# A graph network's two layers on one core: TensorE's steps ordered behind the counting, and the opening loads reordered

## The chip, the cores and the metric

The kernel runs on one core of a Trainium2 chip. The metric is the device time of one execution in microseconds (us). Before the change three executions took 1819.74, 1822.57 and 1822.67 us; the median is 1822.57. The engines are named as in the profile: PE (TensorE, matrix products), DVE (VectorE), ACT (ScalarE), POOL (GpSimd, which issues the indirect loads) and SP (which issues most other transfers).

## The reference

The input is a graph of 2500 nodes with 1024 features each, and 80,000 edges sorted by destination. Two layers follow each other, each with a residual:

```
h   = relu(layernorm(x))
x   = x + segment_sum((h @ W0)[src] * edge_weight[:, None], dst)
h   = relu(layernorm(x))
deg = 1 + number of edges of each dst;   n = deg ** -0.5
x   = x + segment_sum over the edges and self loops of n[dst] * n[src] * (h @ W1.T + b)[src]
```

The first layer needs a gather of rows by `src`, a weight per edge, and a sum by `dst`. The second needs only how often each pair (dst, src) occurs, since its weight is a product of a factor per row and a factor per column.

## The kernel before

**Tiles and blocks.** Nodes are cut into 20 tiles of 128 rows. Edges of a destination tile are cut into blocks of 128: TILE_BLOCKS gives 146 for tile 0, 62, 48, 41 for tiles 1 to 3, down to 10 for tile 19, 675 in all.

**Opening (L149 to L351).** w0 is loaded by eight 512 KB transfers from ACT's queue (L170). Rows of x and columns of its transpose xT come from SP (L145, L154). For each node tile `transposed_rows` takes mean and variance (L126, L128), subtracts the mean from xT through a small product (L160 to L163) and applies ReLU (L164). Beside it a chain of small steps on DVE, PE and POOL finds where each tile's edges start (`heads` L179, L203, L209, L220), gathers the edges by block (`got` L245), transposes them (L263), finds each block's first row (L288, L289) and makes `low` and `key`, the two numbers of an edge from which it is counted.

**Support (L450 to L469).** For each of the 20 node tiles, 16 products with w0 (L453), a scaling by ACT (`row`, L467) and a store to `support` in DRAM (L468).

**Counting (`count_group`, L361 to L402).** For each block DVE makes two one-hot matrices (`oh_low` L380, `oh_key` L382) and PE multiplies them (L384): the counts of source rows against a short window of destination rows, of WINDOWS columns for each source tile. Two to four blocks make a group, and DVE adds the group's result into the tile of counts (L391) at a position read from memory. For the four tiles with most edges (DENSE = 4) ACT also makes three weighted one-hots per block (`wl`, L388), PE multiplies those (L395), and DVE adds them into a dense matrix of edge weights (L398). When a tile is complete it is added to `total` (L401) and stored to DRAM (`cnat`, L402). A new tile of counts is zeroed by ACT (L366; dense L370); there are three buffers of counts, four of each one-hot (pool `ohs`, L115), and two PSUM tiles `cb` for the groups.

**First layer's sums (L501 to L530).** Destination tiles are taken in the order ORDER = 3, 4, 5, 6, 2, 7, 8, 9, 1, ... The four dense ones multiply their dense matrix with rows of `support` read by SP (`multiplied`, L526, L528). The others (`gathered`) take, block by block, 128 rows gathered by POOL (L506), a one-hot (L510), the weighted rows split into two parts (`hi` on ACT L512, `lo` on DVE L514), and four products (L518). Each tile is finished while the next one runs (`finish`, L484 to L499): residual, norm, transposition (L478), 16 products with w1 (L453 again), bias and store.

**Second layer (L580 to L617).** All rows are split into `hi` and `lo`, and each tile's counts, read back transposed (L593), are multiplied with them: 1600 products (L613).

**What sets the order.** The program is written in one order, and a scheduler places the instructions on each engine by data dependences, buffers and its own costs; each engine then runs its list in that order. Where counting is put among the other work is decided in the source by a small model: `clock` holds a time for PE, DVE and ACT, `takes` adds the cost of a step, and `count` (L434), called after each step, adds groups until DVE or ACT would be later than PE. Two lists wait for it: groups of the dense tiles and groups of the others. `least` sets how many blocks of the second may still be open.

Of the kernel before, what the change touches and what calls it, by code (L numbers as in the profile page):

```python
# [9 lines left out]
F32 = mybir.dt.float32  # L10
# [24 lines left out]
LEAD = 4.0  # L35

# [4 lines left out]
def direct(  # L41
# [73 lines left out]
    ohs = first.enter_context(tc.tile_pool(name="ohs", bufs=4))  # L115
    cpool = first.enter_context(tc.tile_pool(name="cpool", bufs=3))
    wpool = first.enter_context(tc.tile_pool(name="wpool", bufs=1, reuse_waits="tile"))
    sup_ctx = tc.tile_pool(name="sup", bufs=3, side="right")
# [30 lines left out]
    def transposed_rows(t):  # L149
        xt = load_rows(t, sup)  # L150
        hT = sup.tile([P, KC, P], F32, name="hT")
        if rows(t) < P:
            nc.gpsimd.memset(hT, 0.0)
        nc.sync.dma_start(hT[:, :, :rows(t)], xT[:, t * P:t * P + rows(t)].rearrange("(k p) n -> p k n", p=P))  # L154
        mv = moments(xt, sup)
# [11 lines left out]
    def load_w(w, engine):  # L167
        ws = [wpool.tile([P, D], F32, name=f"w{k}") for k in range(KC)]
        for k in range(KC):
            engine.dma_start(ws[k], w[k * P:(k + 1) * P, :])  # L170
            yield ws

    for w0_sb in load_w(w0, nc.scalar):
        pass
    ready = {t: transposed_rows(t) for t in range(2)}


    heads = prep.tile([BP, BC, 1], I32, name="heads")
    nc.sync.dma_start(heads, dst.rearrange("(p c e) -> p c e", p=BP, e=P)[:, :, 0:1])  # L179
# [63 lines left out]
    for c in range(QC):  # L243
        n = min(P, NBP - c * P)
        nc.gpsimd.indirect_dma_start(  # L245
            out=got[:n, c].rearrange("p e q -> p (e q)"), out_offset=None, in_=table,
            in_offset=bass.IndirectOffsetOnAxis(ap=edge_i[:n, c:c + 1], axis=1))
    got_f = prep.tile([P, 2, QC, P], F32, name="got_f")
# [30 lines left out]
    for t in range(2, NT):  # L279
        n = TILE_BLOCKS[t] // 2  # L280
        v = second[:, K0[t] - K0[2]:K0[t] - K0[2] + 2 * n].rearrange("p (n g) -> p n g", g=2)
        nc.gpsimd.memset(v[:, :, 1], 1.0)
    first_row = prep.tile([P, NBP], F32, name="first_row")
    for a in range(0, NBP, 4 * P):
# [4 lines left out]
        nc.vector.tensor_scalar(first_row[:, a:a + n], ps[:, :n], 0.0, float(P - 1), op0=ALU.max, op1=ALU.min)  # L289
# [65 lines left out]

    bases = {}
    dense = {}
    counts = {}
    AW = P + 28

    def count_group(t, g, a, b):  # L361

        w = WINDOWS[t][1]
        if t not in counts:
            counts[t] = cpool.tile([P, NT, AW], F16, name="counts")
            nc.scalar.copy(counts[t].rearrange("p t w -> p (t w)"), zero.to_broadcast([P, NT * AW]))  # L366
            nc.vector.tensor_copy(counts[t][:, t, :rows(t)], ident[:, :rows(t)])
            if t < DENSE:
                dense[t] = dpool.tile([P, NT, P + 12], F32, name="dense")
                nc.scalar.copy(dense[t].rearrange("p t w -> p (t w)"), zero.to_broadcast([P, NT * (P + 12)]))  # L370
# [588 lines left out]
```

## Time and profile before

| what | us |
|---|---|
| median of three executions | 1822.57 |
| profiled execution, its own time | 1826.62 |
| its span, first to last instruction | 1824.6 |
| first product L453 / first counting product L384 | 23.5 / 77.3 |
| last weighted one-hot L388 (ACT) | 411 |
| first dense product L528 / first gathered product L518 | 465.6 / 545.3 |
| last product with w1, about | 1437 |
| busy: PE, DVE, ACT, POOL | 1692.6, 1214.6, 911.3, 500.2 |

The table is read as a row of stages: opening, support with counting, first layer's sums, second layer. The span and the events are of the profiled execution, whose time is 4 us above the median. A busy share over the whole span mixes stages with different limits, and the busy time of PE contains records of products that stand in its pipeline and wait.

### The profile page before, as it was taken

How to read it: one execution, taken by the hardware profiler on the slowest of the kernel's cores; microseconds unless marked ns; L12 is line 12 of the kernel's file. 1: busy time of each engine (PE TensorE's matmuls, PEld its weight loads, DVE VectorE, ACT ScalarE, POOL GpSimd, SP SyncE). 2: the span in 40 equal slices, each digit the busy share in tenths (PEclk: the TensorE clock that was granted, in tenths of full speed). 3: DMA queues.
4: the chain of work that ended last, by engine and by line, in shares of the span. 5: the costliest groups of instructions: out<-in, count | busy, mean ns of one | idle time of the engine just before them, and what ended most of it. 6: DMA issues, size and time to landing. Idle time of an engine off the chain costs nothing. (4 is left out here: it accounts for less than half of the span.)

```text
span 1824.6 us, 21434 instructions
## 1 busy us (share of the span) xinstructions
PE 1692.6 (93%) x6506; PEld 1047.4 (57%) x6506; DVE 1214.6 (67%) x3031; ACT 911.3 (50%) x1475; POOL 500.2 (27%) x437
## 2 busy tenths in 40 slices
PE   3899999999869999899999999998999899999998
PEld 1455555554326555466545555455655468888886
DVE  4777766679879998899979999588886330000000
ACT  2499888893117774276625665156654431111110
POOL 2000000000027771277515674166662000000000
PEclk9999999999878999999999999999999999999999
DMA  9123311114759999789978999889885784242420
GB/s 316 52 73 93 108 56 59 47 31 138 264 150 321 377 351 331 216 308 325 345 243 280 325 322 325 261 297 314 307 294 180 210 210 107 81 109 79 113 61 32
DMA packets 216179, 369.97 MB, mean 203 GB/s; under 512 B 115534, under 2 KB 135000, under 8 KB 216054
## 3 DMA queue, kind: packets, MB, share of 16 engines
q0 software_dynamic: 54832, 199.25, 31.5%
q1 hardware_dynamic: 160070, 165.06, 29.0%
q10 hardware_dynamic: 1152, 4.19, 0.7%
q8 instruction: 54, 0.88, 0.2%
q14 instruction: 71, 0.58, 0.1%
HBM read 300.79 MB, written 54.56 MB: 195 GB/s over the span
## 5 line engine op out<-in xcount | busy, mean ns | idle before, releaser
L506 POOL DMA_INDIRECT msg<-support,src_p x378 | 486.1, 1286 | 505.5 <-PE mm L528 126.7
L512 ACT ACTIVATE hi<-msg,wgt_p 128x1024 fp32r<-128x1024 f32 x378 | 423.4, 1146 | 276.3 <-PE mm L518 191.0
L514 DVE SCALAR_TENSOR_TENSOR lo<-msg,wgt_p,hi 128x1024 fp32r<-128x1024 f32 x378 | 476.6, 1280 | 49.6 <-ACT hi L512 47.5
L453 PE MATMUL mm<-w,hT 128*128 128x512 f32 x640 | 321.7, 612 | 1.1 <-ACT hT L164 1.1
L518 PE MATMUL mm<-lo,oh_r 128*128 128x512 f32 x756 | 282.5, 456 | 33.4 <-DVE lo L514 33.3
L518 PE MATMUL mm<-hi,oh_r 128*128 128x512 f32 x756 | 298.1, 477 | 15.9 <-DVE oh_r L510 8.3
L453 PE MATMUL mm<-w,vT 128*128 128x512 f32 x640 | 307.4, 596 | 0.0
L388 ACT ACTIVATE wl<-oh_low,wpart 128x128 bf16<-128x128 bf16 x891 | 267.2, 388 | 21.2 <-PE cb L395 16.1
L613 PE MATMUL mm<-lo,bT 128*128 128x512 f32 (+1 forms) x800 | 248.4, 393 | 3.5 <-DVE lo L587 3.1
L613 PE MATMUL mm<-hi,bT 128*128 128x512 f32 (+1 forms) x800 | 247.7, 392 | 4.1 <-ACT bT L595 2.0
L601 DVE SCALAR_TENSOR_TENSOR rows<-mm,dis,rows 128x1024 f32<-128x1024 f32 x20 | 25.6, 1283 | 308.0 <-PE mm L613 308.0
L518 PEld LDWEIGHTS mm<-lo,oh_r 128*128 128x128 f32 x756 | 141.3, 199 | 117.2 <-DVE lo L514 75.0
L518 PEld LDWEIGHTS mm<-hi,oh_r 128*128 128x128 f32 x756 | 148.7, 202 | 103.4 <-issue 40.3
L382 DVE TENSOR_SCALAR oh_key<-iota,key 128x200 bf16<-128x200 f16 (+13 forms) x675 | 189.7, 292 | 22.5 <-PE cb L395 22.1
L380 DVE TENSOR_SCALAR oh_low<-iota,low 128x128 bf16<-128x128 f16 x675 | 162.8, 251 | 34.4 <-PE cb L384 19.1
L595 ACT CAST bT<-cT 128x2560 fp32r<-128x2560 f16 x20 | 46.6, 2335 | 261.5 <-PE mm L613 257.7
L453 PEld LDWEIGHTS mm<-w,vT 128*128 128x128 f32 x640 | 121.2, 190 | 89.7 <-issue 75.5
L613 PEld LDWEIGHTS mm<-lo,bT 128*128 128x128 f32 (+1 forms) x800 | 149.6, 188 | 40.3 <-DVE lo L587 9.4
L613 PEld LDWEIGHTS mm<-hi,bT 128*128 128x128 f32 (+1 forms) x800 | 150.3, 189 | 37.8 <-ACT hi L585 2.5
L391 DVE TENSOR_TENSOR counts<-cb,counts 128x220 f32 (+13 forms) x296 | 138.7, 468 | 45.2 <-PE cb L384 38.2
L528 PE MATMUL mm<-msg,dense 128*128 128x512 f32 (+1 forms) x320 | 158.8, 610 | 7.6 <-DMA msg<-support 7.6
L384 PE MATMUL cb<-oh_key,oh_low 128*128 128x200 bf16 (+13 forms) x675 | 148.4, 294 | 18.6 <-DVE oh_key L382 16.3
(139 smaller groups left out, 1079.5 us busy)
## 6 DMA issues: line engine op xcount, KB each, us to landing
msg<-support SPq DMA_DIRECT2D x76, 512.0 KB, 6.0
xt<-in_x SPq DMA_DIRECT2D x38, 512.0 KB, 4.0
cnat<-counts SPq DMA_DIRECT2D x20, 640.0 KB, 4.7
x_d<-xt SPq DMA_DIRECT2D x20, 512.0 KB, 5.4
hid_d<-hn SPq DMA_DIRECT2D x20, 512.0 KB, 5.4
rows<-hid_d SPq DMA_DIRECT2D x20, 512.0 KB, 4.7
rows<-x_d SPq DMA_DIRECT2D x20, 512.0 KB, 4.5
hT<-in_xT SPq DMA_DIRECT2D x19, 512.0 KB, 3.8
```

Of the source, the lines that this page charges most:

```text
L380: nc.vector.tensor_scalar(oh_low, iota16[:, :P], low[:, k:k + 1], None, op0=ALU.is_equal)
L382: nc.vector.tensor_scalar(oh_key[:, :NT * w], iota16[:, :NT * w], key[:, k:k + 1], None, op0=ALU.is_equal)
L384: nc.tensor.matmul(cb[:, :NT * w], oh_low, oh_key[:, :NT * w], start=(k == a), stop=(k == b - 1))
L388: nc.scalar.activation(wl[:, i, :], oh_low, AF.Copy, scale=wpart[:, i, k:k + 1])
L391: nc.vector.tensor_tensor(to, cb[:, :NT * w].rearrange("p (t w) -> p t w", w=w), to, op=ALU.add)
L453: nc.tensor.matmul(mm[:, h, :], vT[:, k, :], ws[k][:, h * H:(h + 1) * H], start=(k == 0), stop=(k == KC - 1))
L506: nc.gpsimd.indirect_dma_start(out=msg, out_offset=None, in_=support, in_offset=bass.IndirectOffsetOnAxis(ap=src_p[:, k:k + 1], axis=0))
L512: nc.scalar.activation(hi, msg, AF.Copy, scale=wgt_p[:, k:k + 1])
L514: nc.vector.scalar_tensor_tensor(lo, msg, wgt_p[:, k:k + 1], hi.bitcast(F32), op0=ALU.mult, op1=ALU.subtract)
L518: nc.tensor.matmul(sums[:, h, :], oh, v[:, h * H:(h + 1) * H], start=(j == 0 and v is hi), stop=(j == n - 1 and v is lo))
L528: nc.tensor.matmul(sums[:, h, :], dense[t][:rows(k), k, :P], msg[:rows(k), h * H:(h + 1) * H], start=(k == 0), stop=(k == NT - 1))
L613: nc.tensor.matmul(mm[:, h, :], bT[:rows(k), k, :], v[:rows(k), h * H:(h + 1) * H], start=(k == ORDER[0] and v is his[k]), stop=(k == ORDE ...
```

## The change

- **Opening loads.** w0 no longer comes from ACT's queue. SP loads `heads` first, then x and xT of tile 0, the first column halves of the eight w0 tiles, x and xT of tile 1, the second halves, and x and xT of tiles 2 and 3. Loads are issued four tiles ahead (`load_tile`), with five buffers for xT and four for x. The program's order has the products of tiles 0 and 1 ahead of the edge transposes.
- **Windows.** A block's first row is held at 128 minus the window's width (`roof`), so that counts need 128 columns where they had 156, and the dense matrices 128 where they had 140. `oh_key` shrinks to 460 columns.
- **Buffers.** The one-hot pool has 8 buffers instead of 4.
- **Order.** `fences` keeps, for each call of `count`, the last counting product so far; `on_pe` orders each later step's product behind the one of five calls ago. The edge is for the scheduler alone; no semaphore comes of it. In `gathered` and `multiplied` the first product of a step carries it.
- **How much is counted when.** Costs in `count_next` and the choice between the two lists change, and counting starts after tile 4 instead of tile 2. In the built order of PE, 66 products L453 stand ahead of the first count (34 before), 500 of the 675 counts ahead of the first dense product (399 before), and 547 ahead of the first gathered one (500 before). The last weighted count stands behind 230 products (282 before).
- **Stores.** A tile of counts is stored six calls of `count` after it is complete, ordered behind the last step's product.

The diff, cut to its core:

```diff
+BEHIND = 5
-    ohs = first.enter_context(tc.tile_pool(name="ohs", bufs=4))
+    ohs = first.enter_context(tc.tile_pool(name="ohs", bufs=8))
-    sup_ctx = tc.tile_pool(name="sup", bufs=3, side="right")
+    sup_ctx = tc.tile_pool(name="sup", bufs=4, side="right")
...
-    for w0_sb in load_w(w0, nc.scalar):
-        pass
-    ready = {t: transposed_rows(t) for t in range(2)}
+    AHEAD = 4
     heads = prep.tile([BP, BC, 1], I32, name="heads")
     nc.sync.dma_start(heads, dst.rearrange("(p c e) -> p c e", p=BP, e=P)[:, :, 0:1])
+    w0_sb = [wpool.tile([P, D], F32, name=f"w{k}") for k in range(KC)]
+    loaded = {}
+    for t in range(AHEAD):
+        loaded[t] = load_tile(t)
+        for k in range(KC) if t < 2 else ():
+            nc.sync.dma_start(w0_sb[k][:, t * H:(t + 1) * H], w0[k * P:(k + 1) * P, t * H:(t + 1) * H])
+    ready = {t: transposed_rows(*loaded.pop(t)) for t in range(2)}
...
+    for t in range(2, AHEAD):
+        ready[t] = transposed_rows(*loaded.pop(t))
+    last_pe = None
+    last_count = None
+    fences = []
+
+    def on_pe(i):
+        nonlocal last_pe
+        last_pe = i
+        if len(fences) >= BEHIND and fences[-BEHIND] is not None:
+            order_behind(i, fences[-BEHIND])
+        return i
+
+    def order_behind(i, other):
+        tc.add_manual_dep(i.ins, other.ins.name,
+                          mybir.DependencyInfo(mybir.DependencyClass.NoSync, mybir.DependencyReason.SCHED_ONLY),
+                          reason="order of the steps")
...
+    for t in range(2):
+        for _ in products(t):
+            pass
...
-        nc.vector.tensor_scalar(first_row[:, a:a + n], ps[:, :n], 0.0, float(P - 1), op0=ALU.max, op1=ALU.min)
+        nc.vector.scalar_tensor_tensor(first_row[:, a:a + n], ps[:, :n], 0.0, roof[:, a:a + n],
+                                       op0=ALU.max, op1=ALU.min)
...
-    AW = P + 28
-            counts[t] = cpool.tile([P, NT, AW], F16, name="counts")
+            counts[t] = cpool.tile([P, NT, P], F16, name="counts")
-                dense[t] = dpool.tile([P, NT, P + 12], F32, name="dense")
+                dense[t] = dpool.tile([P, NT, P], F32, name="dense")
...
-            nc.sync.dma_start(cnat[:, t].rearrange("k p d -> p k d"), counts[t][:, :, :P])
+            to_store.append([6, t])
...
-            takes(0.5 * n, (one + 0.25) * n + 2 * add, 0.92 * n)
+            takes(0.5 * n, 1.2 * (one * n + 2 * add), 0.92 * n)
-            takes((0.05 + 0.0005 * wide) * n, (one * n + add) * 1.3)
+            takes((0.05 + 0.0005 * wide) * n, 1.2 * (one * n + add))
...
+    def store_counts(late=True):
+        for entry in to_store:
+            entry[0] -= 1
+        while to_store and (to_store[0][0] <= 0 or not late):
+            t = to_store.pop(0)[1]
+            i = nc.sync.dma_start(cnat[:, t].rearrange("k p d -> p k d"), counts[t])
+            if late:
+                order_behind(i, last_pe)
+
     def count(pe=0.0, v=0.0, s=0.0, least=None):
+        fences.append(last_count)
         takes(pe, v, s)
+        store_counts()
...
-            dense_first = to_count[0] and (not to_count[1] or clock[S] <= clock[V] + LEAD / 2)
+            dense_first = to_count[0] and (not to_count[1] or clock[S] <= clock[V])
...
-        for _ in product(hT, w0_sb, mm):
-            (count if t >= 2 else takes)(1.75)
+        for _ in products(t):
+            (count if t >= 4 else takes)(1.75)
```

## The prediction

> **What bounds the kernel now.** I read the slices of the page first, because no single share describes a kernel with stages.
>
> ```profile
> PE   3899999999869999899999999998999899999998
> DVE  4777766679879998899979999588886330000000
> ACT  2499888893117774276625665156654431111110
> PEclk9999999999878999999999999999999999999999
> ```
>
> PE is nearly always "busy", which says little: records of a waiting matmul count too. What changes is who else is full. ACT is full in slices 3 to 9 (of 45.6 us), DVE from 10 to 15, and both dip in 11 and 12, where the granted clock falls to 0.7. The last eight slices are the final products L613, which the change leaves alone.
>
> Next I cut the span at events of the timeline: first counting matmul (77.3 us), last weighted one-hot `wl` (411), first dense product L528 (465.6), first gathered product L518 (545.3).
>
> ```profile
> core 0: us, PE busy (x) PEld busy (x) DVE busy (x) ACT busy (x) POOL busy (x), PEclk, DMA share, GB/s
> 0.00:77.30 77.30, 44.24 (x104) 19.93 (x105) 48.42 (x223) 21.33 (x22) 13.14 (x58) 0.93 0.64 218
> 77.30:411.00 333.70, 331.23 (x1726) 191.07 (x1725) 232.94 (x925) 308.54 (x934) 0.95 (x1) 1.00 0.21 64
> 411.00:465.60 54.60, 47.01 (x168) 19.46 (x166) 53.13 (x223) 14.21 (x11) 0.00 (x0) 0.94 0.52 158
> 465.60:545.30 79.70, 63.39 (x181) 24.09 (x181) 65.77 (x255) 13.46 (x6) 8.94 (x8) 0.80 0.63 208
> 526.80:545.30 18.50, 10.21 (x24) 2.51 (x24) 16.70 (x61) 2.79 (x1) 0.00 (x0) 0.50 0.27 64
> 545.30:704.00 158.70, 148.70 (x516) 93.13 (x515) 156.89 (x253) 116.46 (x109) 112.96 (x91) 0.95 0.94 345
> 965.00:1136.00 171.00, 159.19 (x543) 99.59 (x541) 159.04 (x267) 109.11 (x105) 112.65 (x82) 0.95 0.90 316
> ```
>
> The reader is to see four limits in turn: PE half empty in the opening; PE and ACT both full while tiles 0 to 3 are counted with weights; DVE full while the rest is counted (53.1 of 54.6 us); DVE, with the DMA at 0.94, in the gathered tiles. In 526.8 to 545.3, PE has nothing but 24 counting records: 26 counts stand in its order ahead of the first gathered product and come at DVE's pace.
>
> Last, the groups of the stretch 77.3 to 411, ACT and then DVE (busy, mean ns | idle before, ended by):
>
> ```profile
> L388 ACT ACTIVATE wl<-oh_low,wpart 128x128 bf16<-128x128 bf16 x886 | 265.7, 388 | 21.2 <-PE cb L395 16.1 <-DVE oh_low L380 3.7 <-PE cb L384 0.8
> L467 ACT ACTIVATE row<-mm,rstd 128x1024 f32<-128x1024 f32 x14 | 15.4, 1100 | 2.2 <-PE mm L453 2.2
> L164 ACT ACTIVATE hT<-hT 128x1024 f32<-128x1024 f32 x14 | 14.6, 1046 | 1.7 <-DVE hT L163 1.6
> ...
> L382 DVE TENSOR_SCALAR oh_key<-iota,key 128x200 bf16<-128x200 f16 (+2 forms) x312 | 76.4, 269 | 22.5 <-PE cb L395 22.1
> L398 DVE TENSOR_TENSOR dense<-cb,dense 128x200 f32 (+1 forms) x102 | 38.0, 372 | 33.7 <-PE cb L395 33.3
> ```
>
> ACT and DVE stand idle for PE's `cb L395`: products of the support stand ahead of the counts in PE's order, and only four one-hot buffers cover the delay.
>
> **The change, part by part.** The built programs of both kernels give the order of instructions on each engine; I count in it and take durations from the profile. A product L453 is two records, 0.86 us (the chain shows four records in 1.72 us).
>
> *Opening.* w0 goes from ACT's queue (eight issues from 0.7 to 16.8 us) to SP's, in sixteen halves of 256 KB, behind `heads`, x and xT of the tile that needs them. SP issues at about 0.42 us each (the xT issue at 1.2 us), so x, xT and eight halves are out by 6 us; at the 350 GB/s of the windows from 5 to 25 us, the 3 MB take 9 us. ACT first runs a table load more (1.3 us, as the one at 17.2), three zeroings (2.3 each), a root and the first ReLU: first product at about 12 us against 23.5. [...] The row has ten 512 KB loads in flight together at a DMA share of 1.0; I go by the row. The edge chain (`heads` to the six `got` gathers) also moves: its matmul L203, at 23.4 us, now stands behind five products and runs at about 16. But its transposes stand behind 32 products, 12 + 32 x 0.86 = 39.5 us (43.6 before), and the first-row product behind 37, about 47 (55.8). Keys and first one-hots follow after 18.6 us as before (55.8 to 74.4): about 66. First `wl` at 67 instead of 75.9. Before the first count PE has done 66 products instead of 34: 27 us of PE work moved into its empty opening.
> First-row reads the `roof` tile as well (two instructions of 0.5 us) and POOL writes it with 20 memsets (`wide`: 20 in some 2 us, idle POOL): under 1 us, and nothing if POOL stays ahead of the gathers.
>
> *Counting with weights.* ACT now does 891 `wl` (267 us), 11 tiles instead of 14 (2.43 each by rows L467, L164, L157: 26.7), four count zeroings at 2.79 x 2560/3120 = 2.29 and three dense at 2.3 (16): 310 us. With 8 buffers the 16.1 us of waiting for PE should go; the other 9 stay; overlap of successive records takes some 6 off (the groups' busy and idle sum to 341 in a stretch of 334). 313 us: last `wl` at 380 instead of 411. Bounds: 298 (start to start, `wl` at 0.291) and 335 (as now). PE needs 164 products (141), 891 x 0.088 and 375 counts (36): 256 us, so ACT is the limit; DVE goes from 233 to some 265 us (68 further counts at 0.6, three tiles' norms less) and loses idle time.
>
> *The rest up to the gathers.* After the last `wl`, 90 products (77 us) and 113 counts (at 0.13: 15) remain: 92, at 96% 95 us; DVE's 113 x 0.61 = 69 lie beside it (0.61: some 90 counts in 54.6 us). Then the 12 us from the last product to the first dense one, which store and load of `support` take now too (453.8 to 465.6): 12 counts fill it. Then 40 dense products and 47 counts, 34.3 + 6.5 = 41, say 43, instead of 79.7: 54 of its 101 counts stand earlier, and the tail of 26 is gone. First gathered product: 380 + 95 + 12 + 43 = 530 instead of 545.3: 15 us won. With the ends: 365 + 92 + 10 + 41 = 508 and 402 + 100 + 12 + 50 = 564.
> The clock is weighed here. [...] the row has it (0.50 in the tail, 0.80 around it). [...] by the row those gathered products wait for DVE's `lo` anyway (156.9 of 158.7 us), so I credit none.
>
> *Gathered tiles.* Counts left after the first gather: 128 instead of 175. The first two gathered stretches and the dense ones between keep theirs within five. The third (965 to 1136) loses 23, 15 us of DVE; DMA at 0.90 allows about 11 of it, I take 8. The last dense stretch loses 17, 2 us of PE; the other dense ones 1. Sum 11; bounds 0 and 18.
>
> *At nothing:* narrower tiles beyond the zeroings (other strides, same elements); the order fence, which puts no wait into the program; w1's loads, as now. **Late stores:** a store moves by six steps behind its sum, on SP; behind it stand msg loads, x1 and hid stores. It frees one of three count buffers, for which ACT's zeroing waits (118.5 us now, mostly with an idle ACT); two zeroings stand among `hi` after the first and second dense tile, but twelve `hi` stand before the first, more than the store's 4.7 us. If that cover fails, some 5 us each.
>
> **Sum.** 15 + 11 = 26 us off the profiled execution (span 1824.6, 1826.6 with what lies around it): span 1798.6, run 1800.6. The median shown lies 4.0 us lower, so 1796.6: 1797.
>
> **Rivals.**
> *ACT gapless and a full PE:* gather at 508, 18 us from the gathered tiles: 55 off, 1768. For it, 95 us of DVE's idle time in that stretch end with PE; against it, ACT never held more than 48.7 us in 50.
> *Only the opening is won* ([...] or `wl` waits as now): last `wl` at 395 to 402, nothing at the first gather, 11 later: 1812; with a gathered stretch held by the DMA, no change at all.
> *Slower:* PE's order lets steps run only five ahead of the counts, and from tile 8 on each support tile carries some 95 weighted one-hots instead of 55. Where one comes late, the product behind it stands too, then `row`, then ACT, which stands behind `row` itself. Place: 67 to 380. Price: each percent of ACT's share is 3.5 us. At 313 + 26 = 339 us the gain is gone: a share of 310 / 339 = 0.91, where the sum above takes 0.99 and the six ACT groups of the stretch now make 315.5 of 333.7, 0.95. At 0.85: 365 us, 1849. For it: DVE's share rises from 0.70 to 0.85, with two PSUM tiles for the counts; against: ACT and PE together reach 0.92 and 0.99 now.
>
> **How the numbers follow.** The sum 0.50, its own range 1783 to 1810; gapless 0.18; opening only 0.17, a third of it within 0.2%; slower 0.15. 0.2% is 3.6 us, about what a measurement of this kernel tells from no change. Faster 0.50 + 0.18 + 0.11 = 0.79, same 0.06, slower 0.15. Eight in ten: from 1767 (about the gapless case's centre) to 1826, which leaves out part of the slower case.
>
> **What would show it.** First product by 13 us, first `wl` near 67, last near 380, first gathered product near 530, no run of counts alone ahead of it, DVE's waits for `cb` well under 95 us, 11 us less between first gather and last product, final products as before (about 386 us). It is wrong if `wl` ends after 400, if ACT's zeroing stands long in front of `hi`, or if the gathered tiles, whose order hardly changes, move by more than 20 us.

## The result and the profile after

The changed kernel takes 1800.0 us (median of four executions, 1795.1 to 1804.5) against 1822.3 beside it: a ratio of 0.988, with a 95% interval of 0.985 to 0.991. The forecast was 1797. The profiled execution took 1796.9 us, its span is 1795.0.

The slices of the page of the changed kernel, 44.9 us each:

```profile
PE   6999999999899999999999999989998999999998
DVE  5887988898698997999988997188886330000000
ACT  3499999961136773276515665166564431111110
PEclk9999999999899999999999999999999999999999
```

ACT is now full without a dip from slice 3 to slice 8, PE has more work in the first slice (6 against 3), and one slice shows a lower clock where three did. Next the stretches of the changed kernel, cut at its own events: first count (86.4 us), last `wl` (374.7), first dense product (482.4), first gathered product (526.5), and 692.3, some 4 us ahead of the first product (696.3) of the dense tile behind the first gathered stretch. In each row an engine's busy us stand with its count of instructions in brackets; PEld is PE loading its weights, PEclk the share of its clock that TensorE was granted.

```profile
core 0: us, PE busy (x) PEld busy (x) DVE busy (x) ACT busy (x) POOL busy (x), PEclk, DMA share, GB/s
0.00:86.40 86.40, 69.19 (x173) 32.10 (x174) 57.62 (x238) 31.50 (x49) 14.35 (x78) 0.96 0.67 220
86.40:374.70 288.30, 280.25 (x1610) 163.96 (x1609) 246.32 (x1051) 288.30 (x901) 0.00 (x0) 0.99 0.22 63
374.70:482.40 107.70, 98.72 (x317) 44.07 (x316) 94.21 (x354) 26.84 (x23) 1.00 (x1) 0.95 0.39 115
482.40:526.50 44.10, 43.62 (x128) 19.95 (x128) 32.50 (x116) 6.95 (x4) 6.57 (x7) 0.96 0.93 309
526.50:692.30 165.80, 150.35 (x526) 95.63 (x524) 156.49 (x250) 117.91 (x110) 114.92 (x92) 0.96 0.94 340
```

Three things are to be seen. The opening is longer than before (86.4 us to the first count, 77.3 before) but PE is busy in 69 us of it, not 44. Between the first count and the last `wl` ACT is busy in every one of 288.30 us. And the 79.7 us from the first dense to the first gathered product have become 44.1, with the clock at 0.96 where it was 0.80.

The groups of the stretch with weighted counts, ACT and then DVE, of the changed kernel (busy, mean ns | idle before, ended by):

```profile
L441 ACT ACTIVATE wl<-oh_low,wpart 128x128 bf16<-128x128 bf16 x891 | 261.9, 410 | 0.0
...
L434 DVE TENSOR_SCALAR oh_key<-iota,key 128x200 bf16<-128x200 f16 (+4 forms) x369 | 97.4, 269 | 3.1 <-PE cb L448 2.8
...
L452 DVE TENSOR_TENSOR dense<-cb,dense 128x200 f32 (+1 forms) x102 | 37.8, 371 | 14.2 <-PE cb L448 13.5
```

The 21.2 us that `wl` waited are 0.0. DVE's waits ahead of `oh_key` and `dense`, nearly all for the weighted products, were 22.5 and 33.7 us and are 3.1 and 14.2.

By event: first gathered product 526.5 us instead of 545.3 (18.8 won), last product of the first layer some 881 us later instead of 892 (11 won), second layer 387.5 instead of 387.3. These are two single executions: the one before lies 4.3 us above its median and the changed one 3.1 below, so they are 29.7 us apart, where the medians are 22.3 apart.

### The profile page after: what moved, and what is told of

It is laid out like the page before. It is cut to its first block, busy times and chain, and to the rows that moved or that the text cites. A ratio compares the mean times of both kernels' runs of the same rounds, so it can differ in the third digit from the quotient of the medians.

```text
span 1795.0 us, 21337 instructions
## 1 busy us (share of the span) xinstructions
PE 1685.8 (94%) x6506; PEld 1047.4 (58%) x6506; DVE 1209.5 (67%) x3031; ACT 900.2 (50%) x1476; POOL 494.5 (28%) x457
## 4 chain that ended last, share of the span: by engine, by line
PE 53%; DVE 7%; DMA 1%; issue 1%; ACT 1%; DVEq 0%; ACTq 0%
PE mm L675 18%; PE mm L570 14%; PE mm L277 13%; PE mm L583 5%; DVE lo L566 3%; DMA rows<-hid_d 1%; PE pT L530 1%; DVE stats L128 1%; DVE xt L539 1%; PE cb L436 1%; DVE lo L649 1%; DVE oh_r L562 0%; ACT hi L647 0%; DVE counts L444 0%; DVE hn L549 0%
## 5 line engine op out<-in xcount | busy, mean ns | idle before, releaser
L558 POOL DMA_INDIRECT msg<-support,src_p x378 | 479.1, 1268 | 493.6 <-PE cb L436 129.0
L277 PE MATMUL mm<-w,hT 128*128 128x512 f32 x640 | 317.4, 608 | 2.4 <-ACT hT L169 2.4
L570 PE MATMUL mm<-hi,oh_r 128*128 128x512 f32 x756 | 291.4, 468 | 15.5 <-DVE oh_r L562 9.9
L441 ACT ACTIVATE wl<-oh_low,wpart 128x128 bf16<-128x128 bf16 x891 | 261.9, 410 | 0.0
L570 PEld LDWEIGHTS mm<-hi,oh_r 128*128 128x128 f32 x756 | 147.2, 199 | 99.4 <-ACT hi L564 41.3
L434 DVE TENSOR_SCALAR oh_key<-iota,key 128x200 bf16<-128x200 f16 (+12 forms) x675 | 193.1, 289 | 3.1 <-PE cb L448 2.8
L444 DVE TENSOR_TENSOR counts<-cb,counts 128x200 f32 (+13 forms) x296 | 138.5, 469 | 59.1 <-PE cb L436 52.8
L675 PEld LDWEIGHTS mm<-lo,bT 128*128 128x128 f32 (+1 forms) x800 | 150.6, 190 | 39.5 <-DVE lo L649 8.1
L432 DVE TENSOR_SCALAR oh_low<-iota,low 128x128 bf16<-128x128 f16 x675 | 164.6, 247 | 6.9 <-PE cb L436 5.5
L583 PE MATMUL mm<-msg,dense 128*128 128x512 f32 (+1 forms) x320 | 150.1, 599 | 5.6 <-DMA msg<-support 5.2
L277 PEld LDWEIGHTS mm<-w,hT 128*128 128x128 f32 x640 | 109.2, 195 | 64.6 <-issue 58.0
```

Of the source, the lines that this page charges most:

```text
L277: on_pe(nc.tensor.matmul(mm[:, h, :], vT[:, k, :], ws[k][:, h * H:(h + 1) * H], start=(k == 0), stop=(k == KC - 1)))
L432: nc.vector.tensor_scalar(oh_low, iota16[:, :P], low[:, k:k + 1], None, op0=ALU.is_equal)
L434: nc.vector.tensor_scalar(oh_key[:, :NT * w], iota16[:, :NT * w], key[:, k:k + 1], None, op0=ALU.is_equal)
L441: nc.scalar.activation(wl[:, i, :], oh_low, AF.Copy, scale=wpart[:, i, k:k + 1])
L444: nc.vector.tensor_tensor(to, cb[:, :NT * w].rearrange("p (t w) -> p t w", w=w), to, op=ALU.add)
L558: nc.gpsimd.indirect_dma_start(out=msg, out_offset=None, in_=support, in_offset=bass.IndirectOffsetOnAxis(ap=src_p[:, k:k + 1], axis=0))
```

## The experiments

Each edit is to the changed kernel unless another is named. Times are medians with the ratio to the kernel before, which ran beside each. The changed kernel's own ratio is 0.988.

### Four buffers, six, and eight in the kernel before

```
-    ohs = first.enter_context(tc.tile_pool(name="ohs", bufs=8))
+    ohs = first.enter_context(tc.tile_pool(name="ohs", bufs=4))
```

> The changed kernel with the one-hot pool at four buffers again, all else kept. Theory A (the eight buffers are what let ScalarE run without a gap between the first and the last weighted one-hot): the `wl` instructions again wait for the products that read them, some 15 to 25 us of idle ahead of them (21.2 us before the change, 0.0 after it), the last `wl` ends near 395 instead of 374.7, and the time is 1812 to 1822. Theory B (the gaplessness comes from the new order of TensorE's steps behind the counting and from the new cost constants): idle ahead of `wl` under 5 us, the last `wl` within 5 us of 374.7, time 1797 to 1805.

The same line with `bufs=6`:

> The changed kernel with six one-hot buffers, between the four that gave 1851 and the eight that give 1800. If each buffer covers so much delay of TensorE (the wait is for the oldest product to be read): ScalarE's idle ahead of `wl` about half of the 33.3 us that four leave, last `wl` near 395 to 400, time 1818 to 1828. If a threshold is crossed (a product's two records of 0.86 us and the three weighted matmuls behind them fit in six): idle under 6 us, 1800 to 1808.

The third takes the kernel before and gives it eight buffers. These don't fit beside the wide tiles (the gather pool then wants 49.5 KB per partition where 42.25 are left), so the 128-wide tiles come along.

```
-    ohs = first.enter_context(tc.tile_pool(name="ohs", bufs=4))
+    ohs = first.enter_context(tc.tile_pool(name="ohs", bufs=8))
...
-    AW = P + 28
+    AW = P
...
+        nc.gpsimd.memset(roof[:, K0[t]:K0[t + 1]], float(P - WINDOWS[t][1]))
```

> The kernel before with eight one-hot buffers and the 128-wide count tiles that make room for them (with the `roof` bound that these need), and none of the rest: old opening, old planner costs, no order behind the counting. Theory A (the buffers are the main part of the gain): ScalarE's 21.2 us of idle ahead of `wl` fall below 5, the last `wl` ends near 376 instead of 411, 100 first-layer products are then left instead of 38, and the first gathered product comes near 530 instead of 545; time 1803 to 1811. Theory B (buffers are worth something only with the new planner costs): last `wl` after 395, time 1815 to 1823.

| one-hot buffers | order and costs as before | as changed |
|---|---|---|
| 4 | 1822 (before) | 1851.2, ratio 1.018 (1.015 to 1.020) |
| 6 | | 1797.6, ratio 0.988 (0.984 to 0.991) |
| 8 | 1806.6, ratio 0.991 (0.989 to 0.992) | 1800.0, ratio 0.988 (0.985 to 0.991) |

With four buffers the changed kernel is slower than the kernel before, which theory A, right in its direction, had not reached: its last `wl` ends at 422.3 us, not 395. The buffers, with the narrow tiles that make room for them, are worth some 16 us under the old order (theory A there held: last `wl` at 366, first gathered product at 534.6); alone they are worth 51 under the new one. ACT's idle time ahead of `wl`, 21.2 us before, is what they change. The first row is the kernel before with eight buffers, the second the changed kernel with four:

```profile
L393 ACT ACTIVATE wl<-oh_low,wpart 128x128 bf16<-128x128 bf16 x891 | 261.8, 392 | 0.0
```

```profile
L441 ACT ACTIVATE wl<-oh_low,wpart 128x128 bf16<-128x128 bf16 x891 | 269.1, 388 | 33.3 <-DVE oh_low L432 17.5 <-PE cb L448 13.5 <-PE mm L277 1.1
```

Six are as good as eight: the gain is complete somewhere between four and six (five was not run), and doesn't grow with each further buffer.

The stretches of 50 us, with the columns of the rows above, show what the order has to do with it: first the kernel before, then the changed one with four buffers, at the same times.

```profile
250.00:300.00 50.00, 49.37 (x249) 27.48 (x248) 33.14 (x133) 46.10 (x138) 0.00 (x0) 1.00 0.19 56
300.00:350.00 50.00, 50.00 (x266) 29.09 (x265) 31.86 (x133) 44.16 (x138) 0.00 (x0) 1.00 0.14 43
```

```profile
100.00:150.00 50.00, 48.17 (x265) 28.06 (x264) 42.75 (x168) 48.07 (x148) 0.00 (x0) 1.00 0.25 77
250.00:300.00 50.00, 41.76 (x225) 24.27 (x223) 38.48 (x157) 41.06 (x120) 0.00 (x0) 0.93 0.20 61
300.00:350.00 50.00, 39.77 (x226) 22.99 (x224) 34.28 (x148) 42.77 (x135) 0.00 (x0) 0.97 0.08 28
```

The second number of a line is PE's busy time. In the kernel before PE stays full when counts are late, because, as we read it, its list has 248 first-layer products between the first count and the last `wl` to fill the waits; the new list has 164, and PE stands with the others (40 of 50 us). The shortage is worst late in the stretch, where tile 0 is counted: its groups have four blocks (its entry of WINDOWS), and a group's weighted products come after all its one-hots, so four buffers hold one group and the next can't start. At 100 us, where groups have two blocks, 48 of 50 us remain. That the group's size is the cause is read from the code and this pattern; no run changed it. Six need not hold two whole groups of four, and yet suffice.

### The order of the steps

```
-        if len(fences) >= BEHIND and fences[-BEHIND] is not None:
-            order_behind(i, fences[-BEHIND])
```

> The changed kernel without the order of TensorE's steps behind the counting of five steps ago (the two lines in `on_pe` are left out), all else kept. If the order carries the gain in the counting stretch or in the gathered tiles: TensorE's first-layer and gathered products run ahead of the counting, ScalarE and VectorE wait more, the counting is left over for the end of the gathered stage, time 1808 to 1825. If it is only a guard that the planner's costs make unnecessary: 1797 to 1805. Rival: the order holds TensorE back, and without it the time is under 1795.

1795.7 us, ratio 0.988 (0.985 to 0.990): no difference from the changed kernel. In the profile the last `wl` stands at 376.6 (374.7), the first gathered product at 527.1 (526.5). The edge that the change is named for wins nothing that can be measured.

### The opening: old loads, and the edge chain first

```
-        for k in range(KC) if t < 2 else ():
-            nc.sync.dma_start(w0_sb[k][:, t * H:(t + 1) * H], w0[k * P:(k + 1) * P, t * H:(t + 1) * H])
...
+    for k in range(KC):
+        nc.scalar.dma_start(w0_sb[k], w0[k * P:(k + 1) * P, :])
```

> The changed kernel with w0 in eight whole 512 KB loads on ScalarE's queue ahead of all else, as before the change; everything after it as changed. By the steps of the prediction the loads by need win 9 to 11 us of the first product: without them the first product comes at about 23.5, the 32 products of tiles 0 and 1 end near 58 instead of 51, the transposes come 7 us later, first `wl` at 85, time about 1807. Rival (the first products are slow anyway[...]): transposes at 51 to 53, time 1798 to 1803.

The new loop stands ahead of the loads of tile 0. The other edit moves the products of tiles 0 and 1 (`for t in range(2): for _ in products(t): pass`) from ahead of the edge transposes to behind the keys.

> The changed kernel with the products of tiles 0 and 1 written behind the edge chain instead of ahead of it, so that on TensorE the transposes of the edges no longer stand behind 32 products. Theory A (the failed step of the opening is the place of the transposes in TensorE's order): transposes at 45 to 46 (when the last of the six gathers is there, 44.8) instead of 51.2, first `wl` at 72 to 73 instead of 78.1, and as ScalarE has no gap after that, everything up to the gathers 5 us earlier: time about 1795. Theory B (66 products must pass TensorE before the first count anyway, and the time up to the gathers is TensorE's): first `wl` earlier, but first gathered product within 2 us of 526.5, time 1798 to 1803.

| us | before | changed | old loads | chain first |
|---|---|---|---|---|
| first product | 23.5 | 13.9 | 24.2 | 13.9 |
| first transpose of edges | 43.6 | 51.2 | 57.8 | 41.3 |
| first one-hot | 74.4 | 75.8 | 81.3 | 75.2 |
| first count on PE | 77.3 | 86.4 | 91.6 | 92.0 |
| first gathered product | 545.3 | 526.5 | 531.7 | 532.6 |
| median (ratio) | 1822 | 1800.0 (0.988) | 1795.9 (0.986) | 1796.4 (0.986) |

The loads by need bring the first product 10 us forward and nothing else that lasts: without them the time is 1795.9, inside the changed kernel's range, although the first gathered product comes 5 us later. In both runs the gathered stage gives that back (875 and 874 us against 881), most of it in its first stretch. Theory A of the second run fails on its own number: transposes 10 us earlier, first one-hot only 0.6 us earlier. VectorE's timeline in the run with the chain first says why:

```profile
45.45 0.29 DVE L302 TENSOR_SCALAR got_f<-got,tile_row 35x128 f32<-35x128 int32 x1 [4.04 <-DMA got<-in_edges,edge_i]
...
68.34 0.84 DVE L385 TENSOR_TENSOR key<-key,inside 128x675 f32<-128x675 f32 x1
69.11 0.45 DVE L393 TENSOR_TENSOR wpart<-wpart 128x297 f32<-128x297 f32 x1
69.49 1.86 DVE L128 BATCH_NORM_STATS2 stats<-xt 128x6 f32<-128x512 f32 x3
...
75.21 0.20 DVE L432 TENSOR_SCALAR oh_low<-iota,low 128x128 bf16<-128x128 f16 x1
```

The last gather is there at 45.4 (44.8 as changed), whatever PE's order; from there DVE needs until 69 for the keys, and then the scheduler gives it norms of later tiles for 6 us. PE's first count waits for the 66 products ahead of it, which now come later (92.0).

### ScalarE relieved

```
-                for i in range(3):
+                for i in range(2):
                     nc.scalar.activation(wl[:, i, :], oh_low, AF.Copy, scale=wpart[:, i, k:k + 1])
+                nc.gpsimd.tensor_scalar(wl[:, 2, :], oh_low, wpart[:, 2, k:k + 1], None, op0=ALU.mult)
...
-            takes(0.5 * n, 1.2 * (one * n + 2 * add), 0.92 * n)
+            takes(0.5 * n, 1.2 * (one * n + 2 * add), 0.62 * n)
```

> The changed kernel with the third weighted one-hot of each block written by GpSimd instead of ScalarE (and the planner told 0.62 us of ScalarE for a block instead of 0.92). Theory A (with eight buffers ScalarE itself is what paces the stretch from the first to the last `wl`, busy 288.3 of 288.3 us): 297 x 0.3 = 89 us go off ScalarE, and VectorE (some 265 us) or TensorE (256) sets the pace: last `wl` of ScalarE near 345 to 355 instead of 374.7, of which up to the first gathered product some 15 to 25 us remain, time 1772 to 1785. Rival 1 (GpSimd's own pace[...]): GpSimd takes over 1 us each or VectorE's one-hots lengthen beyond 0.27 us; the stretch stays at 297 us or grows; time 1800 to 1840. Rival 2 (TensorE's total up to the gathers is what counts): last `wl` early, first gathered product still within 4 us of 526; time 1797 to 1803.

1790.3 us, ratio 0.982 (0.980 to 0.985). The last `wl` of ACT ends at 299.4, 75 us earlier, and the first gathered product comes at 521.6, 5 us earlier. Theory A has the first half right and the second wrong; by the event rival 2 is nearest (it allowed 4 us), while the time lies between what the two said. This is the study's main finding: a full ACT was not what the gathers waited for. The kernel before with eight buffers says the same: its last `wl` ends at 366.2, 8 us ahead of the changed kernel's, and its first gathered product comes 8 us later. The stretches of this run, cut at first count, last `wl`, first dense and first gathered product:

```profile
86.50:299.40 212.90, 202.57 (x1383) 136.89 (x1382) 193.84 (x818) 195.01 (x599) 180.90 (x285) 1.00 0.18 55
299.40:469.80 170.40, 161.20 (x529) 73.56 (x527) 143.04 (x537) 36.73 (x35) 3.94 (x6) 0.98 0.37 111
469.80:521.60 51.80, 48.48 (x141) 21.02 (x142) 41.17 (x150) 9.16 (x5) 8.38 (x8) 0.93 0.88 289
```

PE is busy in 95% of each of the first two (97 and 92% as changed: 280.25 of 288.30, 98.72 of 107.70). When `wl` is done sooner, fewer products lie beside it (102 in PE's list instead of 164) and more are left behind it (152 instead of 90). PE's list up to the first gathered product changes little. At the prediction's prices it is, from the first count on, 254 products and 40 dense ones at 0.86, 891 weighted matmuls at 0.088 and 547 counts at about 0.11: 391 of the 440 us. The rest, some 50 us, is the 17.5 us in which PE stands, and busy time above these prices that isn't taken apart; about 12 of the 50 lie between the last product and the first dense one. GpSimd's help takes off 5. That PE's list sets the event is thus a sum and not an experiment: no run took work off PE alone, and DVE is busy in 91% of this run's first stretch. What would take off more stays open.

### Stores as before

```
-            to_store.append([6, t])
+            to_store.append([0, t])
+            store_counts(late=False)
```

> The changed kernel with every count tile stored as soon as it is complete, as before the change, and not six steps later behind TensorE's last step. If the late store is what made the `counts` zeroing of ScalarE wait for the store (4.63 us in the first gathered tile, and the seven waits of 70.4 us in all that the page lists): first gathered tile 160 to 162 us instead of 165.8, time about 1792 to 1797. If the late store is free or helps (the store stays behind the loads that the products need): the same 1797 to 1803, or later by up to 5 us because 2.6 MB of stores now meet the `msg` and gather transfers.

1798.0 us, ratio 0.987 (0.986 to 0.989): the same. The first gathered stretch is 162.6 us instead of 169.8 (the expectation's 165.8 is its part up to 692.3), near what was expected, but the first gathered product comes at 534.0 instead of 526.5: near the end of the dense tile PE waits 4.2 us for a `msg` load. SP issues nothing from 500.0 to 508.9, in front of a store whose tile is still being counted, with six `msg` loads behind it. The changed kernel has this store behind all but one of its loads (508.2), and the DMA is full (second row) where it was half empty (first row, stores early):

```profile
500.00:515.00 15.00, 15.00 (x48) 6.97 (x47) 12.64 (x44) 1.22 (x1) 0.95 (x1) 1.00 0.53 165
```

```profile
500.00:515.00 15.00, 14.53 (x47) 6.83 (x46) 13.92 (x53) 1.94 (x2) 1.89 (x2) 1.00 0.97 326
```

What the early store wins in the gathered stretch goes ahead of it: the late store trades one wait for another. The wait that it brings is in the changed kernel's ACT timeline:

```profile
547.59 2.32 ACT L418 CAST counts<-zero 128x2560 f16<-128x2560 f32 x1 [4.63 <-DMA cnat<-counts]
549.82 2.19 ACT L564 ACTIVATE hi<-msg,wgt_p 128x1024 fp32r<-128x1024 f32 x2
```

The store was issued at 531.7, behind the store of x1, with the DMA at 0.94, and the zeroing that waits for it began 16 us later; the median landing of these stores is 5.6 us as changed and 4.7 before.

### Counts left for the gathered tiles

```
-            takes(0.5 * n, 1.2 * (one * n + 2 * add), 0.92 * n)
+            takes(0.5 * n, (one + 0.25) * n + 2 * add, 0.92 * n)
...
-            takes((0.05 + 0.0005 * wide) * n, 1.2 * (one * n + add))
+            takes((0.05 + 0.0005 * wide) * n, (one * n + add) * 1.3)
...
-            dense_first = to_count[0] and (not to_count[1] or clock[S] <= clock[V])
+            dense_first = to_count[0] and (not to_count[1] or clock[S] <= clock[V] + LEAD / 2)
...
-            (count if t >= 4 else takes)(1.75)
+            (count if t >= 2 else takes)(1.75)
```

> The changed kernel with the planner's old costs and choice, and counting from tile 2 on; loads, buffers, order behind the counting and late stores as changed. 128 + 53 = 181 counts are left behind the first gathered product instead of 128, and 104 products instead of 90 behind the last `wl`. If these costs carry the 11 us of the gathered tiles: gathered stage 890 to 893 us instead of 881, time 1808 to 1816. If the gathered stage is held by the transfers and VectorE's own work, not by the counts left: 881 to 884, time 1798 to 1804.

```
-            takes((0.05 + 0.0005 * wide) * n, 1.2 * (one * n + add))
+            takes((0.05 + 0.0005 * wide) * n, 1.5 * (one * n + add))
```

> The changed kernel with one planner cost raised (a block of the unweighted counts at 1.5 instead of 1.2 times its VectorE time), so that 179 counts are left behind the first gathered product instead of 128; opening, buffers and the 90 products behind the last `wl` as changed. Theory A (TensorE paces the part up to the gathers, and the first gathered stretch, held by its gathers, has room for the counts): 51 counts at 0.11 to 0.13 us of TensorE come off, first gathered product at 520 to 521 instead of 526.5, gathered stage 878 to 884 us as before, time 1791 to 1796. Theory B (each count left behind costs VectorE's 0.61 us there, as the prediction reckoned for its 11 us): first gathered product at 520, but the gathered stage 888 to 900 us, time 1801 to 1812.

> The third weighted one-hot on GpSimd (which gave 1790) together with the raised cost of the run beside it, 183 counts left behind the first gathered product instead of 130: the version that should beat both kernels if both readings hold. Theory A (TensorE paces the part up to the gathers, counts left are free): first gathered product 6 us earlier than the 521.6 of the GpSimd run alone, gathered stage 880, time 1783 to 1787. Theory B (counts left cost VectorE's time): 1791 to 1800.

The table follows the gathered stage through its stretches, each from its first product to that of the next, with the counts that PE runs in it in brackets; g is gathered, d dense.

| us (counts) | g1 | d2 | g2 | d3 | g3 | d4 | g4 | first g1 | end | median |
|---|---|---|---|---|---|---|---|---|---|---|
| before | 163.8 (14) | 59.0 (58) | 142.0 (9) | 58.1 (56) | 170.1 (21) | 51.9 (17) | 246.8 | 545.3 | 1437 | 1822 |
| changed | 169.8 (14) | 57.1 (54) | 139.2 (11) | 57.2 (49) | 164.6 (0) | 48.7 (0) | 244.2 | 526.5 | 1407 | 1800.0 |
| old costs | 161.4 (14) | 57.2 (60) | 138.2 (13) | 57.8 (54) | 165.8 (19) | 52.6 (21) | 246.3 | 531.5 | 1411 | 1803.8 |
| more left | 163.7 (18) | 56.3 (52) | 138.6 (13) | 56.8 (46) | 173.9 (21) | 54.2 (29) | 245.7 | 518.6 | 1408 | 1792.4 |
| GpSimd | 164.9 (8) | 59.3 (60) | 140.1 (12) | 57.6 (50) | 165.6 (0) | 48.6 (0) | 244.4 | 521.6 | 1402 | 1790.3 |
| GpSimd, more left | 164.2 (20) | 55.8 (53) | 145.7 (14) | 56.3 (44) | 175.5 (21) | 54.6 (31) | 244.4 | 505.4 | 1402 | 1791.7 |

With old costs the ratio is 0.991 (0.987 to 0.995), with more left 0.982 (0.981 to 0.984), with both edits 0.982 (0.981 to 0.983). The old costs give a gathered stage of 879 us with 181 counts in it, where the changed kernel has 881 with 128: the theory that these costs, and with them the fewer counts left, carry the 11 us fails in this run. The kernel before with eight buffers agrees: 175 counts left and a gathered stage of 885 us. Leaving more brings the first gathered product forward by 8 us (16 with GpSimd), where 51 counts (53) make some 6 us of PE's list; the third stretch and the last dense tile then give back 9.3 and 5.5 us (with GpSimd 9.9 and 6.0, and 5.6 in g2). The medians of the last three can't be told apart. For the run alone theory A has the time, theory B the gathered stage (889), and the first gathered product comes 1.4 us earlier than either said. The combination beats neither of its parts. 1790 to 1792 is the best seen, 8 to 10 us under the changed kernel; with more left, alone or with GpSimd, the interval ends below 0.985, where the changed kernel's begins, and with GpSimd alone it ends there.

From the first count to the first gathered product, with GpSimd and then with more left as well:

```profile
86.50:521.60 435.10, 412.25 (x2051) 231.47 (x2050) 378.06 (x1504) 240.89 (x637) 193.23 (x298) 0.98 0.34 105
```

```profile
86.20:505.40 419.20, 402.06 (x1999) 229.18 (x1997) 345.05 (x1373) 234.06 (x634) 191.94 (x298) 0.98 0.33 103
```

PE is 10.2 us less busy and stands 5.7 us less, and DVE is 33 us less busy. The 16 us are more than 53 counts weigh on PE, so PE's list alone doesn't set the event here; DVE may have a part, which no run separates.

### Without `lo`

```
-            lo = gpool.tile([P, D], F32R, name="lo")
-            nc.vector.scalar_tensor_tensor(lo, msg, wgt_p[:, k:k + 1], hi.bitcast(F32),
-                                           op0=ALU.mult, op1=ALU.subtract)
-            for v in (hi, lo):
+            for v in (hi,):
```

> The changed kernel with `lo` and its two products left out of the gathered tiles: part of the result's precision is left out, so its time is not that of the whole computation. 477 us of VectorE and 285 us of TensorE go out of the gathered stage. If VectorE paces the gathered tiles, as the prediction put it for its 11 us: the gathered stage falls from 881 by well over 100 us. If the gathers themselves (378 x 512 KB, DMA share 0.94, GpSimd's 1.27 us for each) pace them, so that 53 counts more or fewer behind the first gather make no difference: it falls by less than 60 us, and the gathered tiles keep 4.5 us or more for each block of 128 edges in their loaded stretches.

A single execution: 1704 us, the gathered stage 788 instead of 881. Neither expectation holds as a whole. The first two stretches do as the second said (172.0 and 131.3 us against 169.8 and 139.2, though the scheduler put 64 and 54 counts into them where there were 14 and 11); the last two as the first said (138.4 and 201.0 against 164.6 and 244.2). First without `lo`, then as changed, 100 us of the first stretch each:

```profile
560.00:660.00 100.00, 81.94 (x240) 42.92 (x239) 64.18 (x220) 71.75 (x69) 58.51 (x61) 0.80 0.94 340
```

```profile
560.00:660.00 100.00, 91.14 (x323) 58.14 (x322) 98.36 (x153) 73.82 (x70) 77.16 (x62) 0.97 0.94 347
```

DVE falls from 98 to 64, and 61 gathers instead of 62 are issued at the same 0.94 of the DMA. DVE and the DMA are both near full there, and taking work off DVE wins nothing in this stretch; that the DMA is what then holds it is read from its share, not tested.

## Why the prediction came out right, and where it did not

**The time: right, partly by luck.** 26 us were forecast, 15 before the gathers and 11 in them; the two profiled executions have 18.8 and 11.0, the medians 22.3 in all. Errors cancel in it: the first `wl` came 11 us later than said, the stretch of `wl` was 16 us shorter, and the 11 us in the gathers aren't shown to come from where it put them.

**Opening: failed at "12 + 32 x 0.86 = 39.5".** The first product came at 13.9, near the 12, but the transposes at 51.2 and the first `wl` at 78.1, not 67. The step gave every product 0.86 us. The changed kernel's PE timeline, and its 5 us stretches, have this:

```profile
25.77 0.59 PE L277 MATMUL mm<-w,hT 128*128 128x512 f32 x1
29.36 0.58 PE L224 MATMUL pT<-spread,ones 20*128 20x20 f32 x2 [3.00 <-DVE spread L222]
29.87 7.30 PE L277 MATMUL mm<-w,hT 128*128 128x512 f32 x10
```

```profile
25.00:30.00 5.00, 2.00 (x7) 0.92 (x5) 0.95 (x6) 0.00 (x0) 0.00 (x0) 0.86 0.80 250
30.00:35.00 5.00, 5.00 (x6) 2.05 (x7) 3.47 (x13) 0.29 (x1) 2.27 (x3) 0.50 0.13 39
```

PE stands 3.0 us in front of a product of the edge chain, which waits for the gather `there` (issued 22.7, landed 28.2), and then runs five products in 7.3 us, at half clock for most of them; the first five had taken 6.6. At 0.86 each five take 4.3. So the later start (1.9), the slow first five (2.3), the stand (3.0) and the slow five behind it (3.0) make 10.2 of the 11.7 us between 39.5 and 51.2. The prediction moved the edge chain's small products behind large ones and priced only the delay of the chain, not the large ones behind the chain. Its second half failed too: even with the transposes at 41 the one-hots don't come before 75, since DVE's own work sets them.

The same paragraph's other number held: 27 us of PE work moved into the empty opening (PE busy 44 to 69 us). The prediction listed it and gave it no term of its own. On PE the 18.8 us add up so: the first count comes 9.1 us later, from there to the first gathered product PE has 19.0 us less to do (422.6 instead of 441.6 us busy) and stands 8.9 us less (17.5 instead of 26.4). That the moved work paid is read from this account and wasn't tested alone; the kernel before with eight buffers has 10.7 of the 18.8 us without it.

**Counting with weights: mechanism right, the term 313 mis-sized.** It measured 296.6, the gapless bound of 298. The remaining 9 us of waits that the sum kept went with the 16, and four buffers bring 33.3 us of waits back. But the label "ACT is the limit" was wrong in its use: ACT was full, and moving a third of the `wl` off it (busy 242.65 instead of 322.09 us between 86.4 and 526.5) moved the first gathered product by 5 us. The sum 380 + 95 + 12 + 43 came to 530 (526.5), but what follows the 380 is long or short as the part beside `wl` is short or long; the sum would better have been made along PE's list, with DVE's beside it.

**Rest up to the gathers: right.** 107 us to the first dense product (107.7), 43 to the gathers (44.1), the tail at a clock of 0.50 gone. Crediting the clock with nothing can't be told from the waits that went with it.

**Gathered tiles: the sum met, its cause not shown.** The third stretch won 5.5 us (8 forecast), the last dense tile 3.2 (2), the other dense tiles 2.8 (1). Not forecast: 2.8 and 2.6 us in the second and fourth gathered stretch, and 6.0 lost in the first. The step that the runs don't bear out is "Counts left after the first gather: 128 instead of 175": with 181 left (old costs) the stage takes 879 us, with 175 (eight buffers in the kernel before) 885, and the third stretch 165.8 and 166.0 with 19 counts in it, where it takes 164.6 with none. Only the last dense tile's gain comes and goes with its counts (51.9 and 52.6 us in these runs). The run with more left (179, 889 us) goes the other way. What else shortened the stage, the narrow tiles or the moments of the transfers, stays open.

**Late stores: failed at "twelve `hi` before the first, more than the store's 4.7 us".** The cover failed, and the price given for that case, 5 us, is what the trace has: 4.63 us of ACT's wait in the middle of `hi`. The 4.7 us were a median over the span; behind this one, issued among the gathers, the zeroing began 16 us after the issue. In runs where this wait is 2.6 and 2.8 us (old loads, chain first) the stretch is 164 to 165 us; that the store makes all of the difference to 169.8 isn't shown.

**Rivals.** The gapless one had ACT right and the time wrong: the last `wl` came 10 us after its 365, since the opening was late, and the gathers 152 us behind that, not 143. The slower one, a late counting that holds the products and so everything, is real: it needs four buffers. That it gives 1851 where 1849 was worked out is chance. The 1849 belong to a share of 0.85 for ACT and a stretch of 365 us; the run has 0.90 and 343.9, for which the same sum gives some 1828, and the late start of `wl` makes 11 of the difference.

**Still open:** which of opening, costs and stores makes the 7 us between the kernel with only buffers and narrow tiles (1806.6) and the whole change (1800.0). Undone one at a time, the loads and stores cost nothing measurable, and the costs 4 us at an interval that includes none.

## What to carry to other kernels

A pool's depth and the order of an engine's list are one decision: an order that takes the filler work out from between dependent products needs more buffers than the old one (1800.0 us with eight), and can be worse than no change without them (1851.2 with four, 1822 before). An engine that is busy all the time (ACT, 288.30 of 288.30 us) isn't yet the bound: take work off it and see whether the event moves (a third of the `wl` off it moved the first gathered product by 5 us), and make the sum along the engine whose list ends at the event. Products moved into an empty opening shorten the list behind it even where nothing there ends sooner (PE busy for 422.6 instead of 441.6 us up to the gathers, from a first count 9.1 us later); what that alone is worth wasn't tested here.

## What the runs showed of the hardware that was not expected

Some instructions of GpSimd and of VectorE were longer in runs in which the other had more to do. In the first gathered stretch, as changed (VectorE busy 160.35 of 169.8 us) and then without `lo` (84.58 of 172.0):

```profile
L558 POOL DMA_INDIRECT msg<-support,src_p x92 | 114.9, 1249 | 41.4 <-issue 23.0 <-DVE lo L566 10.1 <-DVE oh_r L562 6.2
```

```profile
L558 POOL DMA_INDIRECT msg<-support,src_p x92 | 88.8, 965 | 68.0 <-ACT hi L564 59.4 <-issue 7.0 <-ACT vT L531 0.9
```

A gather holds GpSimd for 1249 ns beside `lo` and 965 without it; that run has one execution, and other work changed with it. In the run with GpSimd's one-hots (GpSimd busy 180.90 us beside them, 0.00 as changed), VectorE's `oh_key` and `oh_low` take 299 and 275 ns in the stretch to the last `wl` (269 and 246 as changed), and GpSimd needs 652 ns for what ACT does in 387. What lengthens them no run shows.

A stand of some 3 us was followed by different clocks. PE waits 3.0 us up to 29.4 us in the changed kernel, and 3.1 us up to 28.9, ahead of the same product, in the run without the order of the steps; the clock from 30 to 35 us is 0.50 in the first (shown above) and 1.00 in the second:

```profile
30.00:35.00 5.00, 5.00 (x14) 2.31 (x13) 3.40 (x13) 1.41 (x2) 2.85 (x3) 1.00 0.24 68
```

Between 5 and 25 us the loads moved 337 to 375 GB/s with w0 in sixteen pieces of 256 KB, and 338 to 391 with w0 in eight of 512 KB (old loads), x and xT among them in both. The rows of the two runs overlap, and no loss by the smaller pieces is to be seen in them.
